# Cross attention's small matmuls on parts of the TensorE array: value products by head in turns, folded queries and text scores by head over 64 rows

## Chip, cores, metric

One core of a Trainium2 chip runs the kernel. The metric is device time in microseconds of one execution, median over runs.

## The reference, cut to what matters

The program is a two-layer block over x of 16 batches x 64 queries x 256 features and a context of 16 x 1601 x 256. In order, each with a residual sum: a deformable cross attention, a self attention, a mixture of 8 experts, a second cross attention, a state space scan, a mixture of 32 experts. Everything is float32. The change lies in the second cross attention alone:

```python
ctx_txt = context[:, :TEXT_LEN, :]            # 77 positions
ctx_img = context[:, TEXT_LEN:, :]            # 1524 positions
q = (x @ Wq).reshape(B, N, HEADS, DIM_HEAD)   # 16 heads of 64
k = (ctx_txt @ Wk).reshape(B, TEXT_LEN, HEADS, DIM_HEAD)
v = (ctx_txt @ Wv).reshape(B, TEXT_LEN, HEADS, DIM_HEAD)
out = _attend(q, k, v)                        # softmax(q k^T / 8) v
k_ip = (ctx_img @ Wk_ip).reshape(B, Li, HEADS, DIM_HEAD)
v_ip = (ctx_img @ Wv_ip).reshape(B, Li, HEADS, DIM_HEAD)
out = out + _attend(q, k_ip, v_ip)
return out @ Wo + bo
```

## The kernel before

Up to about 750 us the kernel projects the context's keys and values of the first attention, writes them to DRAM and gathers samples from them. From 753 us on the second cross attention runs (class `Cross`) and carries nearly all other stages beside it as "side" work: generators of the self attention, the first experts, the scan (`Ssm`) and the routing, of which a piece is issued at fixed places of each step. It ends at about 2690 us; the rest of the second experts follows. The order on PE, DVE and ACT is the order in which the program issues the instructions (`manual_schedule`); `tick` counts estimated microseconds of the program, not of the chip, to pace gathers.

The cross attention takes 128 steps (`step`), one for each batch b (16) and pair of heads hp (8). 128 columns of a step are 2 heads x 64 queries. The keys of the image positions are never projected. Instead the query is folded with the key weights, and the folded query is multiplied with the context itself:

- `queries` (L1009 on) projects the queries of two batches and writes them to `qbd`, a tile of 128 rows (two heads x 64 features) by [hp, batch of the two, head, query]. Each head writes only its own 64 rows (L1029); the other 64 rows of its columns stay zero from a memset (L1652). A matmul over 128 rows and 128 columns of it thus gives both heads at once.
- `fold(n)` (L1060 to L1072) makes the folded query of step n: for each of the two halves k of the 256 features one matmul (L1069), stationary 128x128 key weights `w`, moving 128 columns of `qbd`. Both halves lie in one PSUM bank `pf`; ACT copies it to `qf` (L1072).
- `step(n)` first issues the scores, `st` (helper `mm`, L88): 12 chunks of 128 positions, 2 matmuls each, in 3 banks of a pool of their own. DVE takes the maximum of each bank (L1144) and joins them (L1146). Between them stand the transposes of the step before last's output (`turn_out`, L153, ACT copy to `ot` L1122), then `out(n - 2)`, the first third of the product of the step before (`product`, L1113: 4 chunks, weights `pt`, moving 257 columns of context `cn`), the transpose of the maxima (L1163), DVE's maximum over it (L1165), side work, the second third, the transpose back (L1173), ACT's copy `mc` (L1175), `fold(n + 2)`, DVE's differences (L1184, L1187) and ACT's exponentials (L1185, L1188), and the last third of the product with its normalisation (L1194, L1196).
- `out(n)` (L1074 to L1089) is the value projection: for each head an accumulation of three matmuls into its own 64 partitions of one bank: text values times text probabilities (`vt`, `ptt`), then the two halves of `wvi` times `ot`. It is done by `mm` (L88), one head after the other. ACT copies the result to `yt` (L1089).
- `text(b, h)` (L1031 to L1048) makes the text scores of four pairs of heads, 32 times in all: four matmuls over 128 rows (stationary `qbd`, moving 77 keys, L1038) into one bank, from which DVE takes maximum (L1042) and difference (L1044); ACT takes the exponential (L1045), DVE normalises (L1046 to L1048). It is called at hp 5 and 6 of each batch, for the next batch. `text_turn` transposes the result a step later (L153, ACT L1058).

The banks of folds, text, transposes, products and side work come from one pool of 4 (`bank`); a new tile waits until the last reader of the tile that had its bank is done. The score banks (`big`) are another pool of 4.

Of the kernel before, what the change touches and what calls it, by code (L numbers as in the profile page):

```python
# [17 lines left out]
P = 128  # L18
B, S, D = 16, 64, 256
M = 1601  # L20
KC = D // P
# [13 lines left out]
H1, HD1, INNER, TEXT = 16, 64, 1024, 77  # L35
# [30 lines left out]
def perceiver_kernel(ctx: ExitStack, tc: tile.TileContext, a: dict, out: bass.AP):  # L66
    nc = tc.nc

    def mk(pool, shape, tag, dtype=F32, bufs=None):
        return pool.tile(list(shape), dtype, tag=tag, name=tag, bufs=bufs)  # L70
# [15 lines left out]
    def mm(o, pairs):  # L86
        for i, (l, r) in enumerate(pairs):
            nc.tensor.matmul(o, lhsT=l, rhs=r, start=i == 0, stop=i == len(pairs) - 1)  # L88
# [53 lines left out]
    def bank():  # L142
        return mk(pmm, [P, 512], "mm")
# [12 lines left out]
    def load(pool, tag, src, shape, bufs=None):  # L156
        t = mk(pool, shape, tag, bufs=bufs)
        nc.sync.dma_start(out=t, in_=src)
        return t
# [57 lines left out]
    qbds = []  # L217
# [51 lines left out]
    for j in range(2):  # L269
        r = slice(j * S, (j + 1) * S)  # L270
# [688 lines left out]
    class Cross:  # L959
# [71 lines left out]
        def text(self, b, h):  # L1031

            if b >= B:
                return
            kt, qbd, bb = self.kt[b], qbds[b // 2 % 2], b % 2
            ps = bank()[:, : 4 * TEXT].rearrange("p (i n) -> p i n", n=TEXT)
            for i in range(4):
                nc.tensor.matmul(ps[:, i, :], lhsT=qbd[:, h * 4 + i, bb].rearrange("p h q -> p (h q)"), rhs=kt[:, h * 4 + i, :],  # L1038
                                 start=True, stop=True)
            sh = [P, 4, TEXT]  # L1040
            mx = mk(small, [P, 4], "tmx")
            nc.vector.tensor_reduce(mx, ps, AX.X, ALU.max)  # L1042
            pe = self.pe[b, h] = mk(self.xp, sh, "pet", bufs=2)
            nc.vector.tensor_tensor(pe, ps, mx.unsqueeze(2).to_broadcast(sh), ALU.subtract)  # L1044
            nc.scalar.activation(pe, pe, AF.Exp)  # L1045
            nc.vector.tensor_reduce(mx, pe, AX.X, ALU.add)  # L1046
            nc.vector.reciprocal(mx, mx)
            nc.vector.tensor_tensor(pe, pe, mx.unsqueeze(2).to_broadcast(sh), ALU.mult)  # L1048
# [11 lines left out]
        def fold(self, n):  # L1060

            if n >= B * NHP:
                return
            b, hp = divmod(n, NHP)
            w = self.w[b, hp // 4]
            rhs = qbds[b // 2 % 2][:, hp, b % 2].rearrange("p h q -> p (h q)")
            pf = bank()
            for k in range(KC):
                nc.tensor.matmul(pf[:, k * P : (k + 1) * P], lhsT=w[:, hp % 4, k * P : (k + 1) * P], rhs=rhs,  # L1069
                                 start=True, stop=True)  # L1070
            qf = self.qf[n] = mk(self.xc, [P, KC, P], "qf", bufs=3)
            nc.scalar.copy(qf.rearrange("p c n -> p (c n)"), pf[:, : KC * P])  # L1072

        def out(self, n):  # L1074

            if n < 0:
                return
            b, hp = divmod(n, NHP)
            t, bb = divmod(b, 2)
            if t not in self.yt:  # L1080
                self.yt[t] = mk(self.xp, [P, NHP, 2, S], "yt", bufs=2)
            ot = self.ot.pop(n)
            py = bank()
            for h in range(2):
                r = slice(h * HD1, (h + 1) * HD1)
                cols = slice(hp * P + h * HD1, hp * P + (h + 1) * HD1)
                mm(py[r, :S], [(self.vt[b][:TEXT, cols], self.ptt[b][:TEXT, hp, r])]
                   + [(wvi[:, k, cols], ot[:, k, r]) for k in range(KC)])
            nc.scalar.copy(self.yt[t][:, hp, bb, :], py[:, :S])  # L1089

        def project(self, t):
# [506 lines left out]
    with tc.manual_schedule(engines={ET.PE, ET.DVE, ET.Activation}):  # L1598
# [21 lines left out]
        for s in range(B * 7 + 1):  # L1620
            run(kv)
            if s >= 1:
                run(early)
            if s == 14:
                pace["open"] = True
            tick(3.9)
            if s >= 18 and next(text, True) is None:
                tick(2.4)
            if s == 60:
                drain(text)  # L1630
                stx.close()
                tc.swap_default_side()
                slp = ExitStack()
                lp = slp.enter_context(tc.tile_pool(name="lp", bufs=2))
                tc.swap_default_side()
                mw = Middle(lp)
                for t0, nt in ((0, TG), (TG, ND0 - TG)):
                    mids += [(4 * (t0 + nt), attention(t0, nt, lp, mw)), (0, middle(t0, nt, lp, mw))]
                late = attention(ND0, 1, lp, mw)
                for k in range(KC):  # L1640
                    nc.vector.tensor_scalar(rws[:, k, :], rws[:, k, :], rsc[:, k : k + 1], None, ALU.mult)
            if lp:
                mid()
                if s < 94:
                    mid()
        drain(kv)
        skv.close()
        wvi = load(xw, "wvi", a["xwvi"].rearrange(kp, p=P), [P, KC, INNER])
# [10 lines left out]
        i = 0  # L1659
# [30 lines left out]
        for t in range(ND0 + 1, NPAIR):  # L1690
            i = (t - ND0) % TG
# [44 lines left out]
        i = 0  # L1736
# [127 lines left out]
```

## Time and profile before

| what | value |
|---|---|
| median of 3 runs | 2980.36 us (2976.62 to 2980.77) |
| the profiled execution | 2978.07 us, its span 2976.4 us |
| PE busy, of the span | 2811.3 us, 94% |
| DVE, ACT, POOL busy | 1626.4, 1071.7, 830.4 us |
| scores L88 st<-qf,cT | 6144 passes, 278 ns each |
| products L1113 | 3072 passes, 385 ns each |
| folds L1069 | 504 + 8 passes, 276 ns each |
| value products L88 | 512 passes mm<-ptt,vt of 246 ns, 1024 mm<-ot,wvi of 222 ns |
| text scores L1038 | 256 passes, 269 ns each |

How to read it: the profile is of one execution on the chip. Groups are named by line, engine and tiles, "out<-in" with buffer numbers left out. PE is the matmul stream, PEld the weight loads that run beside it. The trace has two matmuls ("passes") and two loads for each float32 matmul of the program, except for transposes, which have one. The ends of matmuls are modelled, so the 278 ns of a pass are its time in flight; where passes follow each other, the distance from start to start says what one costs. In a timeline a line is start, duration, engine, source line, tiles, shape and count; "[idle <- releaser]" is idle time before it and what ended it. A line of the waits is "engine line <- what it waited for: us in total, times, longest".

### The profile page before, as it was taken

What the parts mean: (1) busy time and instruction counts of PE and PEld (TensorE: products, weight loads), DVE (VectorE), ACT (ScalarE), POOL (GpSimd) and SP (SyncE); (2) the same over time, 40 slices, a digit from 0 to 9 for tenths busy, and PEclk for the clock granted to TensorE, in tenths of its full rate; (3) what the DMA queues carried; (4) which work ended last, traced back from release to release, by engine and by line L of the source; (5) the groups of instructions that cost most, each with busy time, mean ns of one, the idle gap of its engine ahead of it and who ended that gap; (6) DMA issues with size and microseconds to landing.
All of it is one profiled execution on the core that took longest, in us unless ns stands there. A gap on an engine that the chain in (4) does not pass through costs nothing.

```text
span 2976.4 us, 46295 instructions
## 1 busy us (share of the span) xinstructions
PE 2811.3 (94%) x17734; PEld 2344.9 (79%) x17734; DVE 1626.4 (55%) x4138; ACT 1071.7 (36%) x2427; POOL 830.4 (28%) x923
## 2 busy tenths in 40 slices
PE   8999999796899988999999999999999999997799
PEld 4554466464788877899999999999999999994687
DVE  3344443533566655332557754686544785655856
ACT  3443433542223443333343332443232443222431
POOL 0677777777771000000101100020000010001723
PEclk9999999998899999999999999999999999999999
DMA  7666766476322101465212111121111221005753
GB/s 218 180 193 201 225 184 195 137 236 183 77 69 63 49 10 41 135 192 167 70 50 80 52 33 52 55 71 55 38 33 47 66 64 51 8 1 161 218 151 110
DMA packets 324853, 313.97 MB, mean 105 GB/s; under 512 B 57989, under 2 KB 275881, under 8 KB 324121
## 3 DMA queue, kind: packets, MB, share of 16 engines
q1 hardware_dynamic: 172137, 213.05, 22.5%
q10 hardware_dynamic: 126928, 63.06, 7.5%
q0 software_dynamic: 25568, 34.91, 5.3%
q8 instruction: 141, 2.31, 0.3%
q14 instruction: 79, 0.65, 0.1%
HBM read 236.31 MB, written 74.62 MB: 104 GB/s over the span
## 4 chain that ended last, share of the span: by engine, by line
PE 76%; DVE 8%; POOL 6%; issue 3%; DMA 3%; ACT 3%; SPq 1%; ACTq 0%; DVEq 0%; POOLq 0%
PE st L88 31%; PE mm L1113 21%; PE mm L88 14%; POOL g L446 6%; PE mm L153 4%; PE mm L1069 2%; DMA g<-tab,ig 2%; DVE hs L1359 1%; PE mm L1099 1%; DVE hc L1364 1%; PE mm L1038 1%; ACT pt L1185 1%; DVE db L1357 1%; DVE mp L1144 1%; PE mm L1163 1%
## 5 line engine op out<-in xcount | busy, mean ns | idle before, releaser
L1113 PE MATMUL mm<-cn,pt 128*128 128x257 f32 (+1 forms) x3072 | 741.6, 385 | 1.2 <-ACT cT L82 1.2
L88 PE MATMUL st<-qf,cT 128*128 128x128 f32 x6144 | 739.9, 278 | 0.0
L88 PEld LDWEIGHTS st<-qf,cT 128*128 128x128 f32 x6144 | 721.3, 194 | 3.3 <-ACT qf L1072 0.2
L446 POOL DMA_INDIRECT g<-tab,ig x640 | 620.2, 969 | 282.1 <-issue 176.9
L1113 PEld LDWEIGHTS mm<-cn,pt 128*128 128x128 f32 (+1 forms) x3072 | 555.4, 190 | 84.6 <-ACT cT L82 2.3
L88 PE MATMUL st<-wkv,cxt 128*128 128x512 f32 (+1 forms) x832 | 377.1, 598 | 1.0 <-ACT cxt L415 1.0
L1144 DVE TENSOR_REDUCE mp<-st 128x128 f32<-128x512 f32 x384 | 260.4, 688 | 214.5 <-PE st L88 214.1
L1184 DVE TENSOR_TENSOR pt<-st,mc 128x512 f32<-128x512 f32 (+1 forms) x384 | 224.2, 639 | 152.2 <-ACT mc L1175 152.2
L88 PEld LDWEIGHTS st<-wkv,cxt 128*128 128x128 f32 (+1 forms) x832 | 149.1, 187 | 157.6 <-issue 155.9
L1185 ACT ACTIVATE pt<-pt 128x512 f32<-128x512 f32 (+1 forms) x384 | 207.5, 588 | 51.9 <-DVE pt L1184 51.6
L399 ACT COPY kv<-st 128x512 f32<-128x512 f32 (+1 forms) x208 | 121.3, 588 | 190.2 <-PE st L88 189.6
L1175 ACT COPY mc<-mm 128x128 f32<-128x128 f32 x128 | 34.2, 267 | 385.3 <-PE mm L1173 384.8
L972 POOL MEMSET cn<- 128x12 f32 x16 | 2.0, 122 | 590.6 <-PE mm L1113 584.1
L1122 ACT COPY ot<-mm 128x256 f32<-128x256 f32 x128 | 47.5, 371 | 311.2 <-PE mm L153 311.1
L1165 DVE TENSOR_REDUCE xmx<-mm 128x1 f32<-128x128 f32 x128 | 37.4, 292 | 193.4 <-PE mm L1163 193.4
L1465 POOL DMA_INDIRECT xb<-xnd,row x55 | 59.6, 1084 | 281.8 <-PE mm L1099 217.8
L1365 POOL TENSOR_TENSOR mn<-mn,hc 128x512 f32<-128x512 f32 x64 | 84.1, 1314 | 173.4 <-DVE hc L1364 165.2
L1089 ACT COPY yt<-mm 128x64 f32<-128x64 f32 x128 | 27.2, 213 | 248.4 <-PE mm L88 248.4
L88 PEld LDWEIGHTS mm<-xt,w 128*128 128x128 f32 x512 | 83.0, 197 | 26.0 <-issue 14.4
L88 PE MATMUL mm<-xt,w 128*128 128x256 f32 (+1 forms) x512 | 94.8, 333 | 3.3 <-DVE act L886 3.3
L1347 POOL MEMSET da<- 128x8 f32 x64 | 7.5, 117 | 319.3 <-ACT da L1346 319.0
L1359 DVE TENSOR_TENSOR_SCAN hs<-da,db 128x512 f32<-128x512 f32 x64 | 79.3, 1239 | 7.0 <-DVE db L1357 0.5
(469 smaller groups left out, 3978.1 us busy)
## 6 DMA issues: line engine op xcount, KB each, us to landing
tab<-kv ACTq DMA_DIRECT2D x48, 1024.0 KB
w<-in_gate SPq DMA_DIRECT2D x66, 512.0 KB
cx<-in_ctx SPq DMA_DIRECT2D x48, 512.0 KB
cn<-in_ctx SPq DMA_DIRECT2D x16, 1408.0 KB
w<-in_lin SPq DMA_DIRECT2D x33, 512.0 KB
wk<-in_xwkiT SPq DMA_DIRECT2D x32, 512.0 KB
wg<-in_guT SPq DMA_DIRECT2D x55, 256.0 KB
g<-tab,ig POOLq DMA_INDIRECT x640
```

The source lines that it names most:

```text
L88: nc.tensor.matmul(o, lhsT=l, rhs=r, start=i == 0, stop=i == len(pairs) - 1)
L153: nc.tensor.transpose(t[:ncol, i, :rows], b, ident[:rows, :rows])
L399: nc.scalar.copy(kv[:w, :, c, :], pk[:w].rearrange("p (h e) -> p h e", h=H0))
L446: nc.gpsimd.indirect_dma_start(out=gf[:, (half * n + s) * 4 * HD0 : (half * n + s + 1) * 4 * HD0], out_offset=None, in_=tables[j], in_offs ...
L1069: nc.tensor.matmul(pf[:, k * P : (k + 1) * P], lhsT=w[:, hp % 4, k * P : (k + 1) * P], rhs=rhs, start=True, stop=True)
L1113: nc.tensor.matmul(po, lhsT=pt[:w, c, :], rhs=cn[:w, c, :], start=c == 0, stop=c == NCH - 1)
L1144: nc.vector.tensor_reduce(mp_[:, i, :], s.rearrange("p c n -> p n c"), AX.X, ALU.max)
L1184: nc.vector.tensor_tensor(o, st[i][:, :m, :], mc.to_broadcast([P, m, P]), ALU.subtract)
L1185: nc.scalar.activation(o, o, AF.Exp)
L1359: nc.vector.tensor_tensor_scan(hs.rearrange("p c n -> p (c n)"), da.rearrange("p c n -> p (c n)"), db.rearrange("p c n -> p (c n)"), 0.0, ...
L1365: nc.gpsimd.tensor_tensor(y, y, hc, ALU.add)
L1465: nc.gpsimd.indirect_dma_start(out=x, out_offset=None, in_=xnd, in_offset=bass.IndirectOffsetOnAxis(ap=tb.row[:, i : i + 1], axis=0))
```

## The change

Three edits. The value products of the two heads are issued in turns, matmul by matmul, instead of head by head. The fold takes each head over its own 64 rows and 64 query columns (4 matmuls in place of 2), into a bank for each head, and ACT copies each bank to its half of `qf`. The text scores take each head over its 64 rows into its 64 partitions (8 matmuls in place of 4), into a bank for each head; ACT copies the two halves to SBUF, and DVE's maximum and difference read that copy. `qbd` and its zeros stay as they are. Lines behind the first edit move down by 5 or more: L1042 becomes L1048, L1069 L1076, L1072 L1080, L1113 L1123, L1144 L1154, L1163 L1173, L1173 L1183, L1175 L1185, L1185 L1195; the value products leave the helper and are L1098, their copy L1099, ACT's text copies L1045.

```diff
--- before.py
+++ after.py
@@ -1033,14 +1033,19 @@
             if b >= B:
                 return
             kt, qbd, bb = self.kt[b], qbds[b // 2 % 2], b % 2
-            ps = bank()[:, : 4 * TEXT].rearrange("p (i n) -> p i n", n=TEXT)
+            pe = ps = self.pe[b, h] = mk(self.xp, [P, 4, TEXT], "pet", bufs=2)
+            pb = [bank()[:, : 4 * TEXT].rearrange("p (i n) -> p i n", n=TEXT) for _ in range(2)]
             for i in range(4):
-                nc.tensor.matmul(ps[:, i, :], lhsT=qbd[:, h * 4 + i, bb].rearrange("p h q -> p (h q)"), rhs=kt[:, h * 4 + i, :],
-                                 start=True, stop=True)
+                for g in range(2):
+                    r = slice(g * HD1, (g + 1) * HD1)
+                    nc.tensor.matmul(pb[g][r, i, :], lhsT=qbd[r, h * 4 + i, bb, g, :], rhs=kt[r, h * 4 + i, :],
+                                     start=True, stop=True)
+            for g in range(2):
+                r = slice(g * HD1, (g + 1) * HD1)
+                nc.scalar.copy(ps[r], pb[g][r])
             sh = [P, 4, TEXT]
             mx = mk(small, [P, 4], "tmx")
             nc.vector.tensor_reduce(mx, ps, AX.X, ALU.max)
-            pe = self.pe[b, h] = mk(self.xp, sh, "pet", bufs=2)
             nc.vector.tensor_tensor(pe, ps, mx.unsqueeze(2).to_broadcast(sh), ALU.subtract)
             nc.scalar.activation(pe, pe, AF.Exp)
             nc.vector.tensor_reduce(mx, pe, AX.X, ALU.add)
@@ -1063,13 +1068,16 @@
                 return
             b, hp = divmod(n, NHP)
             w = self.w[b, hp // 4]
-            rhs = qbds[b // 2 % 2][:, hp, b % 2].rearrange("p h q -> p (h q)")
-            pf = bank()
+            pf = [bank(), bank()]
+
             for k in range(KC):
-                nc.tensor.matmul(pf[:, k * P : (k + 1) * P], lhsT=w[:, hp % 4, k * P : (k + 1) * P], rhs=rhs,
-                                 start=True, stop=True)
+                for h in range(2):
+                    r = slice(h * HD1, (h + 1) * HD1)
+                    nc.tensor.matmul(pf[h][:, k * S : (k + 1) * S], lhsT=w[r, hp % 4, k * P : (k + 1) * P],
+                                     rhs=qbds[b // 2 % 2][r, hp, b % 2, h, :], start=True, stop=True)
             qf = self.qf[n] = mk(self.xc, [P, KC, P], "qf", bufs=3)
-            nc.scalar.copy(qf.rearrange("p c n -> p (c n)"), pf[:, : KC * P])
+            for h in range(2):
+                nc.scalar.copy(qf[:, :, h * S : (h + 1) * S], pf[h][:, : KC * S].rearrange("p (k q) -> p k q", q=S))
 
         def out(self, n):
 
@@ -1081,11 +1089,13 @@
                 self.yt[t] = mk(self.xp, [P, NHP, 2, S], "yt", bufs=2)
             ot = self.ot.pop(n)
             py = bank()
-            for h in range(2):
-                r = slice(h * HD1, (h + 1) * HD1)
-                cols = slice(hp * P + h * HD1, hp * P + (h + 1) * HD1)
-                mm(py[r, :S], [(self.vt[b][:TEXT, cols], self.ptt[b][:TEXT, hp, r])]
-                   + [(wvi[:, k, cols], ot[:, k, r]) for k in range(KC)])
+
+            for i in range(1 + KC):
+                for h in range(2):
+                    r = slice(h * HD1, (h + 1) * HD1)
+                    cols = slice(hp * P + h * HD1, hp * P + (h + 1) * HD1)
+                    x, y = (wvi[:, i - 1, cols], ot[:, i - 1, r]) if i else (self.vt[b][:TEXT, cols], self.ptt[b][:TEXT, hp, r])
+                    nc.tensor.matmul(py[r, :S], lhsT=x, rhs=y, start=i == 0, stop=i == KC)
             nc.scalar.copy(self.yt[t][:, hp, bb, :], py[:, :S])
 
         def project(self, t):
```

## Prediction

> **What bounds the kernel now.** I read the windows first, then the waits, then the chain of work that ended last. All edits lie in the cross attention, which runs from 753 us to about 2690 us. The windows give busy time by stretch, in the order PE, PEld, DVE, ACT, POOL, then the clock:
>
> ```profile
> 1500.00:1700.00 200.00, 199.51 (x1494) 182.81 (x1493) 140.54 (x278) 71.38 (x180) 21.13 (x33) 1.00 0.18 54
> 1700.00:1900.00 200.00, 200.00 (x1484) 184.01 (x1483) 107.43 (x273) 70.91 (x163) 1.58 (x4) 1.00 0.16 51
> ```
>
> PE has no idle time there, its clock is granted in full, ACT is busy for 36%, DVE for 54 to 70%. PE's longest waits between 800 and 2690 us:
>
> ```profile
> PE mm L1163 <- DVE mp L1146: 7.5, 9, 2.5
> PE mm L153 <- DVE xn L103: 7.2, 2, 6.9
> ```
>
> All of PE's listed waits there come to some 35 us in 1890, so other engines can hide under 2% of a change on PE. The chain says the same of the whole span:
>
> ```profile
> PE 76%; DVE 8%; POOL 6%; issue 3%; DMA 3%; ACT 3%; SPq 1%; ACTq 0%; DVEq 0%; POOLq 0%
> ```
>
> So a nanosecond more or less of PE's sequence in a step of this loop is, 126 to 128 times, a nanosecond of the span; ACT and DVE matter only where PE comes to wait for them. As a busy PE in this profile only says that matmuls are in flight, I work with distances between starts.
>
> **The fold, before.** One float32 matmul stands in the trace as two passes, each a weight load and a matmul. The PE timeline around one fold:
>
> ```profile
> 1508.07 0.27 PE L1173 MATMUL mm<-ident,xmx 128*128 128x128 f32 x1
> 1508.17 0.61 PE L1069 MATMUL mm<-qbd,wk 128*128 128x128 f32 x4
> 1508.62 0.60 PE L1113 MATMUL mm<-cn,pt 128*128 128x257 f32 x2
> ```
>
> From the transpose (L1173) to the first pass are 108 ns, from there to the next product 446 ns (medians over the folds): 4 passes of 111 ns. Nothing drains, as all these matmuls take the whole 128x128 array.
>
> The change issues 8 passes in place of 4, each with 64 rows and 64 moving columns, but still 128 weight columns. Does a half-wide moving operand shorten a pass? The old text scores answer it: 77 moving columns over 128 weight columns.
>
> ```profile
> 1451.39 1.01 PE L1038 MATMUL mm<-kt,qbd 128*128 128x77 f32 x8
> 1452.24 0.60 PE L153 MATMUL mm<-ident,pet 128*77 128x128 f32 x4
> ```
>
> 8 passes in 849 ns, 106 ns each, hardly less than the 111 ns with 128 moving columns: the load of 128 weight columns sets the pass. Rows don't shorten a load either: 64 columns over 77 rows take 55 ns from start to start, over 128 rows 55 to 60. So a pass of the new fold still costs 106 ns, and the two heads must run side by side on the two halves of the array for 8 passes to cost what 4 did. Whether they do, and what it costs to enter and leave that shape, the trace shows at another place, the value products (L1088), which take 64 columns of the array at a time:
>
> ```profile
> 1501.77 0.83 PE L88 MATMUL st<-qf,cT 128*128 128x128 f32 x6
> 1502.53 0.33 PE L88 MATMUL mm<-ptt,vt 77*64 77x64 f32 x2
> 1502.70 0.22 PE L88 MATMUL mm<-ot,wvi 128*64 128x64 f32 x1
> 1502.70 0.27 PE L88 MATMUL mm<-ptt,vt 77*64 77x64 f32 x1
> 1502.76 0.22 PE L88 MATMUL mm<-ot,wvi 128*64 128x64 f32 x1
> 1502.81 0.22 PE L88 MATMUL mm<-ptt,vt 77*64 77x64 f32 x1
> 1502.81 0.45 PE L88 MATMUL mm<-ot,wvi 128*64 128x64 f32 x6
> 1503.19 0.70 PE L1113 MATMUL mm<-cn,pt 128*128 128x257 f32 x2
> ```
>
> Two things are to be seen. First, the second head starts at 1502.70 while the first still runs, and both then take 57 ns a pass: the column halves work at once. Second, a change of shape drains. The last full-array matmul starts at 1502.327; the first load of the 64-column shape follows at 1502.531, 204 ns later where 111 is the rule: 93 ns of drain, and the load (53 ns for 64 columns) is no longer hidden. On the way out the last 64-column matmul starts at 1503.043 and the product's load at 1503.193: 150 ns where 57 is the rule, again 93, and then the product's load of 107 ns stands bare (its second pass starts 321 ns after the first, not 217). The 32x32 matmuls at 1174.87 show the like: 100 ns from a 17-column matmul to the next full-array load.
>
> **The fold, after.** The new fold (L1076) changes shape in its middle of a full-array sequence, in and out, in all 126 folds of the loop. Counted from the transpose's start: load at 204, first matmul at 204 + 107 = 311, three more passes of 106 = 629, the other head beside it some 6 ns later (the two column halves at L291 start at 18.105 and 18.111), out after 53 + 93 = 781, the product's load of 107 = 888. Before it was 108 + 446 = 554. So **+334 ns a step, x126 = +42 us**.
> Bounds: a row split alone (64x128) is not in this trace, all switches shown change the columns too. If it drains nothing, the fold costs 4 x 106 in place of 446, -22 ns x126 = -3 us; nothing shorter, since 128-column loads set the pass. If it drains and the halves don't overlap, 4 more passes of 106 = +53 us on top, +95 us. I take +42, as every switch of shape in the trace drains.
> Here the Trainium skill speaks against the change: TensorEngine Tiling (Array Packing), Key Properties, says that a change of tiling mode, not of tile, drains TensorE, and it lists 64x128 as a mode. By the rule the sum holds +42; by these rows alone a row split could be -3.
>
> **The value products, after.** The heads alternate. In the old order the second head's first load comes 12 records behind the first head's and starts 171 ns later; at L291 it is 4 records behind and starts 6 ns later. The new order puts it 4 records behind. So the block shrinks from 340 + 171 = 511 ns (first to last start) to about 346: **-165 ns x128 = -21 us**. Nothing less than one head's own chain of 340 is possible, so -22 us is the floor; if the alternation brings nothing, 0. The switches on both sides stay.
>
> **The text scores, after.** 32 blocks, PE at 64 rows x 64 columns: 8 passes of 68 ns (77 columns of 0.83 ns, plus 4) = 544, plus 93 + 53 in and 93 + 107 out = 890 against 849: +41 ns x32 = **+1 us**. Without overlap +544 x32 = +17 more; without drains -10.
> ACT gets two copies of 64x308 (L539, the same width at 128 rows, takes 417 ns), and DVE's maximum (L1048) now waits for them: 0.83 us x32 = 27 us if all of it showed. Behind it on DVE stand the rest of the text's chain and the next step's maxima (L1154), for which PE waits at L1173 only some 8 us later. I take 0: that distance is the cover. DVE pays the same on SBUF as on PSUM (L1046 474 ns, L1042 474 ns). The two banks that wait for ACT are wanted next by the transposes of os, 16 passes later.
>
> **The exit of the fold.** Two copies to qf instead of one:
>
> ```profile
> L1072 ACT COPY qf<-mm 128x256 f32<-128x256 f32 x128 | 47.8, 373 | 18.6 <-PE mm L1069 7.9
> L1175 ACT COPY mc<-mm 128x128 f32<-128x128 f32 x128 | 34.2, 267 | 385.3 <-PE mm L1173 384.8
> L539 ACT COPY kts<-mm 128x308 f32<-128x308 f32 x32 | 13.3, 417 | 21.8 <-PE mm L88 21.8
> ```
>
> 2 x 267 - 373 = +161 ns, x128 = 21 us of ACT, behind which the exponentials (L1195) wait. They need DVE's first difference, which ends 1.30 us after the transpose; the second copy ends at about 1.38. Their result is wanted a whole step later. I take 0; at worst 21 us. In the built order the second bank of 6 folds was last read by the copy of mc (L1185), so those wait some 0.4 us: **+2 us**. SP and POOL issue the same transfers; one load of kt moves behind one of wq at the start, at no price, as both are loaded a step ahead.
>
> **Sum.** +42 - 21 + 1 + 2 = +24 us. The profiled execution took 2978.07 us (span 2976.4); the median of the three runs is 2.3 us above. 2978 + 24 + 2 = **3004 us**.
>
> **Rivals.**
> 1. The row split does not drain (faster). Mechanism: a 64-row load enters beside running full-array matmuls. Place: both ends of L1076. The fold falls from +42 to -3, the sum to -21, **2959 us**. It decides once entering and leaving cost under 170 ns a step together instead of 334 + 22. For it: no row of before has a pure row split. Against: each switch that it has drains. Chance 0.13.
> 2. The halves of rows don't overlap, or their weight loads go one after the other. The fold +95, the text +18: 3004 + 53 + 17 = **3074 us**; with the fold alone 3057. For it: overlap is shown for column halves only. Against: the Trainium skill, TensorE: Matmul & The Clock Gate, The mechanism, says that loads overlap running matmuls when their row groups differ; no run here shows that yet. Chance 0.2.
> 3. The copies on ACT come into PE's way: up to 27 + 21 us, **3025 to 3052 us**. For it: DVE is 70% busy in some stretches, so its slack is finite. Against: PE's 35 us of waits. Chance 0.1.
> 4. Draining, but with the next load already taken in: both 107 ns fall away, the fold is +15 us, the sum about -3: **2977 us**, no change. Against: the bare load behind every value product. Chance 0.07.
>
> **How the numbers follow.** My forecast has 0.5, with its own range 2993 to 3018; rivals 0.13, 0.2, 0.1 and 0.07. About 0.2% (6 us) is what a measurement of this kernel can tell from no change. Faster: rival 1, 0.13. Same: rival 4, 0.07. Slower: the rest, 0.8. The range reaches from rival 4 to rival 2 and leaves rival 1 out: 2976 to 3075.
>
> **What would show it.** Fold: from the transpose (L1183) to the first load 204 ns, to the next product's bare load some 780 ns; with 110 instead of 204, rival 1. Inside the fold two passes should start within some 10 ns of each other; passes 106 ns apart, eight in a row, are rival 2. Value products (L1098): both heads within 10 ns, 346 ns from first to last start. PE's waits for DVE at L1173 should stay near 10 us; 30 or more is rival 3. I am wrong altogether if a split pass takes another time than a full one.

## The result, and the profile after

| | before | after |
|---|---|---|
| median of 4 runs | 2979.03 us (2976.62 to 2980.77) | 3014.24 us (3009.39 to 3016.42) |
| the profiled execution | 2978.07 us, span 2976.4 | 3009.39 us, span 3007.7 |
| ratio after/before, 95% interval | | 1.0117 [1.0099, 1.0134] |

The change makes the kernel slower by some 35 us (30 to 40); forecast were 3004 us. The loop of the cross attention, taken from the first transpose back (L1183) to the last, grew by 36.5 us, so all of it lies there.

The windows of the kernel after, in the order PE, PEld, DVE, ACT, POOL, clock:

```profile
1500.00:1700.00 200.00, 197.97 (x1541) 176.42 (x1540) 134.04 (x270) 78.77 (x203) 18.42 (x30) 1.00 0.19 57
1700.00:1900.00 200.00, 200.00 (x1530) 179.04 (x1529) 109.29 (x267) 70.99 (x177) 4.28 (x7) 1.00 0.13 41
```

PE is still the bound and its clock still granted in full, but in the first stretch it is idle for 2 us, where it was 0.5. Passes rose from 1494 to 1541 and 1484 to 1530 per 200 us although the kernel is slower: there are more of them, of half the rows. The weight loads are busy for less time: after a change of shape nothing is loaded ahead.

**A fold.** PE, and then the weight loads, around one fold of the kernel after (start, duration, what):

```profile
1531.24 0.27 PE L1183 MATMUL mm<-ident,xmx 128*128 128x128 f32 x1
1531.44 0.66 PE L1076 MATMUL mm<-qbd,wk 64*128 64x64 f32 x8
1532.03 0.92 PE L1123 MATMUL mm<-cn,pt 128*128 128x257 f32 x3
```

```profile
1531.02 0.13 PEld L1183 LDWEIGHTS mm<-ident,xmx 128*128 128x128 f32 x1
1531.44 0.52 PEld L1076 LDWEIGHTS mm<-qbd,wk 64*128 64x128 f32 x8 [0.28 <-issue]
1532.03 0.73 PEld L1123 LDWEIGHTS mm<-cn,pt 128*128 128x128 f32 x4
```

Before, the fold's load ran under the transpose. Now the load unit stands idle for 0.28 us, and the first load of 64 rows begins 199 ns after the transpose has begun and its matmul 201 ns (medians over the loop). The eight matmuls come as four pairs: 7 ns apart within a pair, and from pair to pair 160, 112 and 112 ns. The last start is 391 ns behind the first one, the product's first pass 202 ns behind that. The whole takes 0.79 us from transpose to product, where it took 0.55.

**The value products**, in turns, of the kernel after:

```profile
1526.62 0.50 PE L88 MATMUL st<-qf,cT 128*128 128x128 f32 x3
1527.04 0.34 PE L1098 MATMUL mm<-ptt,vt 77*64 77x64 f32 x4
1527.21 0.40 PE L1098 MATMUL mm<-ot,wvi 128*64 128x64 f32 x8
1527.54 0.70 PE L1123 MATMUL mm<-cn,pt 128*128 128x257 f32 x2
```

Both heads' text products now stand side by side ahead of both heads' image products. From first to last start it is 347 ns (511 before); the switch in (205 ns) and out (152 ns) stays.

**A text step.** What the prediction took at nothing shows on DVE. First DVE in the same step of the kernel before (step 45, hp 5), from the end of the product of one step to the maxima of the next:

```profile
1553.78 0.49 DVE L1196 TENSOR_SCALAR os<-mm,xrc 128x256 f32<-128x256 f32 x1
1554.18 0.47 DVE L1042 TENSOR_REDUCE tmx<-mm 128x4 f32<-128x308 f32 x1
...
1560.17 0.29 DVE L1146 TENSOR_TENSOR mp<-mp 128x128 f32<-128x128 f32 x1
1560.95 0.29 DVE L1165 TENSOR_REDUCE xmx<-mm 128x1 f32<-128x128 f32 x1 [0.48 <-PE mm L1163]
```

then ACT and DVE in it, after:

```profile
1563.63 1.64 ACT L1195 ACTIVATE pt<-pt 128x512 f32<-128x512 f32 x3 [2.27 <-DVE pt L1194]
1565.18 0.29 ACT L1198 ACTIVATE pt<-pt 116x128 f32<-116x128 f32 x1
1565.38 0.83 ACT L1045 COPY pet<-mm 64x308 f32<-64x308 f32 x2
```

```profile
1564.97 0.48 DVE L1206 TENSOR_SCALAR os<-mm,xrc 128x256 f32<-128x256 f32 x1
1566.24 0.47 DVE L1048 TENSOR_REDUCE tmx<-pet 128x4 f32<-128x308 f32 x1 [0.79 <-ACT pet L1045]
...
1568.93 0.68 DVE L1349 TENSOR_TENSOR mt<-xc,dt 128x512 f32<-128x512 f32 x1
1569.54 0.61 DVE L1351 TENSOR_SCALAR mn<-xc,dp 128x256 f32<-128x256 f32 x2
...
1572.30 0.29 DVE L1156 TENSOR_TENSOR mp<-mp 128x128 f32<-128x128 f32 x1
```

and last PE's transpose of the maxima, before and after:

```profile
1560.61 0.30 PE L1163 MATMUL mm<-ident,mp 128*128 128x128 f32 x1 [0.24 <-DVE mp L1146]
```

```profile
1572.74 0.30 PE L1173 MATMUL mm<-ident,mp 128*128 128x128 f32 x1 [1.01 <-DVE mp L1156]
```

The two copies stand on ACT behind the exponentials; DVE sits idle for 0.79 us until they are done. From the start of its normalisation to the text's maximum it is 1.27 us (1564.97 to 1566.24), where it was 0.40 (1553.78 to 1554.18), and the scores' maxima come later by about as much. The side work of the scan (L1349, L1351) stands between and leaves no slack. PE waits 1.01 us for the maxima; in the same step before it waited 0.24. Over the loop, DVE's waits at the text (engine, line <- what it waited for: us, times, longest) and PE's longest wait, after:

```profile
DVE tmx L1051 <- ACT pet L1050: 24.0, 30, 1.9
DVE tmx L1048 <- ACT pet L1045: 23.5, 27, 1.6
```

```profile
PE mm L1173 <- DVE mp L1156: 13.3, 12, 3.4
```

The first stood at 15.8 us before, the second had no counterpart, the third stood at 7.5. PE's listed waits in the loop come to 46 us, 36 before.

### The profile page after: what moved, and what is told of

Read it like the earlier page. It is cut to its first block, busy times and chain, and to the rows that moved or that the text cites. A ratio compares the mean times of both kernels' runs of the same rounds, so it can differ in the third digit from the quotient of the medians.

```text
span 3007.7 us, 48085 instructions
## 1 busy us (share of the span) xinstructions
PE 2836.2 (94%) x18502; PEld 2322.7 (77%) x18502; DVE 1632.8 (54%) x4138; ACT 1107.6 (37%) x2619; POOL 825.3 (27%) x923
## 4 chain that ended last, share of the span: by engine, by line
PE 74%; DVE 9%; POOL 5%; DMA 4%; ACT 4%; issue 3%; SPq 0%; ACTq 0%; DVEq 0%; POOLq 0%
PE st L88 30%; PE mm L1123 21%; PE mm L88 12%; POOL g L446 5%; PE mm L153 4%; PE mm L1076 2%; PE mm L1098 2%; DMA g<-tab,ig 2%; DVE hs L1369 1%; DVE mp L1154 1%; ACT pt L1195 1%; PE mm L1109 1%; DVE hc L1374 1%; PE mm L1173 1%; DVE db L1367 1%
## 5 line engine op out<-in xcount | busy, mean ns | idle before, releaser
L1123 PE MATMUL mm<-cn,pt 128*128 128x257 f32 (+1 forms) x3072 | 752.4, 388 | 0.0
L1123 PEld LDWEIGHTS mm<-cn,pt 128*128 128x128 f32 (+1 forms) x3072 | 554.5, 190 | 90.1 <-issue 1.2
L1154 DVE TENSOR_REDUCE mp<-st 128x128 f32<-128x512 f32 x384 | 259.5, 688 | 212.3 <-PE st L88 212.1
L1195 ACT ACTIVATE pt<-pt 128x512 f32<-128x512 f32 (+1 forms) x384 | 207.2, 588 | 32.8 <-DVE pt L1194 30.1
L1185 ACT COPY mc<-mm 128x128 f32<-128x128 f32 x128 | 34.1, 266 | 387.5 <-PE mm L1183 387.0
L1175 DVE TENSOR_REDUCE xmx<-mm 128x1 f32<-128x128 f32 x128 | 37.4, 292 | 174.7 <-PE mm L1173 174.7
L1099 ACT COPY yt<-mm 128x64 f32<-128x64 f32 x128 | 27.2, 213 | 228.8 <-PE mm L1098 228.8
L1076 PEld LDWEIGHTS mm<-qbd,wk 64*128 64x128 f32 x1008 | 68.4, 187 | 36.2 <-issue 31.3
```

The source lines that it names most:

```text
L1076: nc.tensor.matmul(pf[h][:, k * S : (k + 1) * S], lhsT=w[r, hp % 4, k * P : (k + 1) * P], rhs=qbds[b // 2 % 2][r, hp, b % 2, h, :], start= ...
L1123: nc.tensor.matmul(po, lhsT=pt[:w, c, :], rhs=cn[:w, c, :], start=c == 0, stop=c == NCH - 1)
L1154: nc.vector.tensor_reduce(mp_[:, i, :], s.rearrange("p c n -> p n c"), AX.X, ALU.max)
L1195: nc.scalar.activation(o, o, AF.Exp)
```

## The experiments

All are built from the kernel before. Each group ran on one chip beside runs of the kernel before, and is compared with those. Only lines that differ are shown, with "..." where some are left out.

### Group 1: each part alone (before: 2975.91 us)

**e1_turns**: only the value products in turns.

```diff
-            for h in range(2):
...
-                mm(py[r, :S], [(self.vt[b][:TEXT, cols], self.ptt[b][:TEXT, hp, r])]
-                   + [(wvi[:, k, cols], ot[:, k, r]) for k in range(KC)])
+            for i in range(1 + KC):
+                for h in range(2):
...
+                    nc.tensor.matmul(py[r, :S], lhsT=x, rhs=y, start=i == 0, stop=i == KC)
```

> The kernel before with the value products in turns alone; fold and text scores as before. My theory (each edit's price is the change of PE's own sequence): from first to last start of a block 347 ns in place of 511, 164 ns x 128 steps = 21 us less, so about 2958 us against 2979. Rival theory A (PE has slack at this place, and what the turns save is waited away at the next transpose of the maxima): under 6 us less, 2973 or more.

Measured: 2957.71 us, ratio 0.9932 [0.9920, 0.9944], -18 us; the loop -18.7 us, -0.164 us a step. So this part alone is a gain, of the size that the start distances gave.

**e2_fold**: only the fold by head.

```diff
...
+                for h in range(2):
...
+                    nc.tensor.matmul(pf[h][:, k * S : (k + 1) * S], lhsT=w[r, hp % 4, k * P : (k + 1) * P],
+                                     rhs=qbds[b // 2 % 2][r, hp, b % 2, h, :], start=True, stop=True)
...
```

> The kernel before with the fold by head over 64 rows alone. My theory: drain in, drain out and one bare load of 107 ns, some 345 ns a step in 126 steps = +43 us, and 2 us for folds that wait for a bank: about 3024 us against 2979. Rival theory B (the fold is nearly free and the loss of the change sits in the text scores and in the copies on ACT): +10 us or less.

Measured: 3015.67 us, ratio 1.0133 [1.0118, 1.0147], +40 us; the loop +37.4 us, +0.34 us in a regular step. In seven steps at hp 2 and 5 it is 0.00; in all seven PE waits for the maxima (L1163) in the kernel before too. The fold alone is dearer than the whole change.

**e3_text**: only the text scores by head, with ACT's two copies.

```diff
...
+                for g in range(2):
...
+                    nc.tensor.matmul(pb[g][r, i, :], lhsT=qbd[r, h * 4 + i, bb, g, :], rhs=kt[r, h * 4 + i, :],
+                                     start=True, stop=True)
+            for g in range(2):
...
+                nc.scalar.copy(ps[r], pb[g][r])
```

> The kernel before with the text scores by head over 64 rows alone. My theory: +37 ns of PE in 32 blocks = +1 us, and +0.77 us in each block after which PE comes to wait for the maxima of DVE, which seemed about half of the 32 in the changed kernel: +10 us together, about 2989 us. Rival theory B: +20 us or more, as the text carries the loss. The prediction as made: +1 us.

Measured: 2993.24 us, ratio 1.0049 [1.0036, 1.0061], +17 us. The loop grew by 20.6 us: 9.2 at hp 5, 8.6 at hp 6, 2.7 at hp 0, all of it in the first step, and at most 0.3 at any other. Not every text step pays: 13 of the 32 did not grow. Its waits, DVE's for the copies and then PE's for the maxima and for a copy of DVE's:

```profile
DVE tmx L1048 <- ACT pet L1045: 23.3, 27, 1.8
```

```profile
PE mm L1168 <- DVE mp L1151: 13.2, 10, 3.2
PE mm L153 <- DVE cT L84: 3.5, 5, 1.9
```

The first two are those of the whole change, to 0.2 us: the chain copies, DVE, maxima, PE comes from this part alone. The third has no counterpart in the kernel before: at hp 6, PE waits for DVE to copy out transposed context (`cT`, L84), a second way in which a late DVE reaches PE.

**e4_fold_exit**: the old fold, but its bank copied by two ACT copies of 128x128.

```diff
-            nc.scalar.copy(qf.rearrange("p c n -> p (c n)"), pf[:, : KC * P])
+            for h in range(2):
+                nc.scalar.copy(qf[:, :, h * S : (h + 1) * S],
+                               pf[:, : KC * P].rearrange("p (k n) -> p k n", n=P)[:, :, h * S : (h + 1) * S])
```

> The kernel before; the fold's matmuls stay on the full array and in one bank, but ACT copies the bank to qf by head in two instructions, as the changed kernel does. My theory (ACT's 161 ns more a step are covered): within 3 us of 2979. Rival theory C (part of the fold's price is ACT's second copy, behind which the exponentials wait): up to 161 ns x 128 = +21 us, 3000.

Measured: 2976.94 us, ratio 1.0006 [0.9995, 1.0018]. The two copies of a step overlap in the trace: together they span 434 ns where one took 373, so ACT is busy for 8 us more in all (1080 for 1072), not for the 21 of the sum. These cost nothing that shows. So e2's +40 is PE's. That e3 pays for the place of its copies, ahead of DVE, is what e6_text_exit tests.

### Group 2: what the price hangs on (before: 2976.54 us)

**e5_fold_pairs**: the folds of two steps together, every second step. As many passes, half as many changes of shape.

```diff
-            if n >= B * NHP:
+            if n >= B * NHP or n % 2:
...
+            for j in range(2):
+                for k in range(KC):
+                    for h in range(2):
...
+                        nc.tensor.matmul(pf[h][:, c * S : (c + 1) * S], lhsT=w[r, (hp + j) % 4, k * P : (k + 1) * P],
+                                         rhs=qbds[b // 2 % 2][r, hp + j, b % 2, h, :], start=True, stop=True)
...
```

> The fold by head over 64 rows, but for two steps at a time in every second step: the same matmuls and copies as in the fold-only kernel, half as many changes of the array's shape. My theory (the price is paid for each change of shape): a pair takes 201 + 838 + 202 + 107 = 1348 ns plus 111 for the step without a fold, against 2 x 554 before: +351 ns a pair, +22 us, some 18 us less than the fold-only kernel (3016). Rival theory D (the price is paid for each pass, 8 small ones in place of 4): no gain by pairing, again +40 us.

Measured: 3000.9 us, ratio 1.0077 [1.0063, 1.0091], +24 us. PE in it:

```profile
2295.44 0.27 PE L1179 MATMUL mm<-ident,xmx 128*128 128x128 f32 x1
2295.64 1.11 PE L1072 MATMUL mm<-qbd,wk 64*128 64x64 f32 x16
2296.68 0.92 PE L1119 MATMUL mm<-cn,pt 128*128 128x257 f32 x3
```

Sixteen matmuls in a block between the same two gaps (201 and 202 ns). Half the switches, little more than half the price: it is paid per change of shape, not per matmul.

**e6_text_exit**: the old text matmuls, one ACT copy of 128x308 to SBUF, DVE reads the copy.

```diff
...
+            nc.scalar.copy(pe, ps)
+            ps = pe
...
```

> The kernel before with its full-array text matmuls in one bank; only the way out is new: ACT copies the bank to SBUF in one instruction of 128x308 and DVE reads that copy. My theory (the text's +17 us is the wait of DVE behind ACT's copies, and PE's wait for the maxima after it): one copy of 0.42 us in place of two of 0.41, so about half, +7 to +10 us, 2985. Rival theory E (the text's loss is PE's: 16 small passes and the change of shape): 0.

Measured: 2983.55 us, ratio 1.0027 [1.0016, 1.0038], +7 us, with PE's instructions as they were. DVE's waits for the copy:

```profile
DVE tmx L1045 <- ACT pet L1042: 13.7, 25, 1.4
```

One copy gives 13.7 us of DVE waiting and +7 us; two give 23.3 us and +17.

**e7_turns_2**: the value products in turns, of two steps at a time, into one bank, with one copy.

```diff
-            if n < 0:
+            if n < 0 or n % 2 != 1:
...
+            for j in range(2):
...
+                for i in range(1 + KC):
+                    for h in range(2):
...
+                        nc.tensor.matmul(py[r, j * S : (j + 1) * S], lhsT=x, rhs=y, start=i == 0, stop=i == KC)
...
```

> The value products in turns, for two steps at a time in every second step, into one bank with one copy; fold and text as before. My theory (each change of shape costs 93 ns and a bare load): a pair costs 1036 ns beyond the sequence without it, two single blocks in turns 2 x 699, so -362 ns a pair, -23 us below the turns-only kernel: about 2935 us. Rival theory A (steps without a block leave DVE less time for the maxima, and PE waits): 2950 or more.

Measured: 2937.56 us, ratio 0.9869 [0.9854, 0.9884], -39 us, the fastest version of all. PE in it, one block of 24 matmuls between two gaps:

```profile
2312.54 0.34 PE L1091 MATMUL mm<-ptt,vt 77*64 77x64 f32 x4
2312.70 0.40 PE L1091 MATMUL mm<-ot,wvi 128*64 128x64 f32 x8
2312.94 0.29 PE L1091 MATMUL mm<-ptt,vt 77*64 77x64 f32 x4
2313.05 0.40 PE L1091 MATMUL mm<-ot,wvi 128*64 128x64 f32 x8
```

It takes 205 ns in, 697 from first to last start, 152 out. Against e1_turns half the changes of shape are gone, worth another 20 us.

**e9_whole_array**: the value products on the whole array, both heads' columns in one matmul; twice the multiplications, half the output block unused, no change of shape; two ACT copies pick the halves.

```diff
+            mm(py[:, :P], [(self.vt[b][:TEXT, cols], self.ptt[b][:TEXT, hp, :])]
+               + [(wvi[:, k, cols], ot[:, k, :]) for k in range(KC)])
             for h in range(2):
...
+                nc.scalar.copy(self.yt[t][r, hp, bb, :], py[r, r])
```

> The value products on the whole array: 3 matmuls of 128 columns for both heads with 128 moving columns, half of whose output (one head's weights times the other head's values) is not used; ACT copies the two halves that are. Twice the multiplications, no change of shape. My theory: 6 passes of 111 = 666 ns beyond the sequence without it, against 864 before and 699 in turns: -198 ns x 128 = -25 us, about 2951 us, some 4 less than the turns-only kernel. Rival theory D (work counts, not changes of shape): no better than before, 2976 or more.

Measured: 2957.78 us, ratio 0.9939 [0.9925, 0.9952], -19 us. PE in it:

```profile
1630.69 0.39 PE L88 MATMUL mm<-ptt,vt 77*128 77x128 f32 x2
1630.92 0.61 PE L88 MATMUL mm<-ot,wvi 128*128 128x128 f32 x4
1631.37 0.82 PE L1113 MATMUL mm<-cn,pt 128*128 128x257 f32 x3
```

Six passes in place of twelve, with ordinary distances of 112 ns at both ends. Regular steps fell by 188 ns, 198 were foreseen; steps that wait for DVE gave less, which is the rest up to the 25 expected. Multiplying the zeros is as fast as leaving them out in turns, within a microsecond (e1_turns, in another group).

### Groups 3 and 4: how far the heads overlap

**e10_fold_heads** (before: 2977.77 us): the fold by head alone, as e2_fold, with the loops exchanged, one head after the other. The lines are shown against e2_fold.

```diff
-            for k in range(KC):
-                for h in range(2):
+            for h in range(2):
+                for k in range(KC):
```

> The fold-only kernel with the loops exchanged: all passes of the first head, then all of the second. My theory (the row halves work at once, as far as PE looks ahead: in the old value products the second head started when the 7th of the 12 records before its own went): the second head's first load is 9th in line and starts some 107 to 160 ns after the first head's, not 7, so the block takes 100 to 155 ns longer in 126 steps: +13 to +20 us over the fold-only kernel, 3029 to 3036 beside 3016 against 2976. Rival theory F (the halves overlap in any order): as the fold-only kernel, 3016. Rival theory G (without turns no overlap at all): 4 more passes of 106, +53 us.

Measured: 3014.24 us, ratio 1.0119 [1.0102, 1.0136], +36 us, and +0.347 us in a regular step where e2_fold had 0.340. The loads of one fold:

```profile
1616.79 0.53 PEld L1071 LDWEIGHTS mm<-qbd,wk 64*128 64x128 f32 x8 [0.28 <-issue]
```

The eight take 0.53 us, 0.52 in turns. The second head's first load starts 12 to 14 ns behind the first head's, although eight records stand ahead of it. I had expected the order to cost as it does in the value products; that fell.

**e11_wait_first**: the value products head by head as before, but the text's matmul last, so that a wait for the transposes stands at the first matmul of each head instead of the second. It ran on another chip, on which both kernels took longer (before: 3296.83 us); it is compared with that alone. In its trace the stage ahead of the cross attention takes some 250 us more than in the profile before.

```diff
-                mm(py[r, :S], [(self.vt[b][:TEXT, cols], self.ptt[b][:TEXT, hp, r])]
-                   + [(wvi[:, k, cols], ot[:, k, r]) for k in range(KC)])
+                mm(py[r, :S], [(wvi[:, k, cols], ot[:, k, r]) for k in range(KC)]
+                   + [(self.vt[b][:TEXT, cols], self.ptt[b][:TEXT, hp, r])])
```

> The kernel before with one head after the other as it was; within a head the text product comes last, so that the wait for ACT's copy to ot stands at the first of the 12 records of the first head and no longer at the third matmul pass. Theory H (PE looks only so far ahead: a load 9th in line was reached at once, one 13th in line is not): the second head starts some 170 ns after the first as before, the time stays at 2977. Rival theory I (the semaphore in the middle of the first head's chain holds up what is behind it): the second head starts within 20 to 60 ns, the block falls from 511 to 360 to 400 ns, -14 to -19 us, 2958 to 2963.

Measured: 3298.6 us, ratio 1.0003 [0.9976, 1.0031]. The weight loads of one block:

```profile
1938.74 0.36 PEld L88 LDWEIGHTS mm<-ot,wvi 128*64 128x64 f32 x6
1938.97 0.14 PEld L88 LDWEIGHTS mm<-ptt,vt 77*64 77x64 f32 x1
```

The first line holds four loads of the first head and, from the fifth on, two of the second head, which starts 171 ns behind, as before. So the wait in the middle was not the reason. With e10_fold_heads: a head whose first load is the 9th record in line starts at once, one whose first load is the 13th doesn't. But the two cases also differ in the kind of split, halves of rows there and halves of columns here, and no run separates this from the number of records. What sets the limit stays open.

## Why the prediction was right, and where a step of it failed

The sign and the size were right, by the mechanism that was given most of the chance. Of the terms of the sum, the text scores were put at next to nothing and cost 17 us; the others came out within 3 us.

- **The fold: right.** Foreseen were 204 ns to the first load, 629 ns to the last start, 781 to the product's load, 888 with the bare load; measured 199, 592, 791 and some 898. That is +340 ns a step for +334, +40 us for +42 by itself. The last start came sooner than foreseen (592 for 629), and the way out took longer: 202 ns from the last start to the product's first pass, where the value products leave their 64-column shape in 152. Both come from where the starts are recorded. In the full-array fold a pass starts 107 to 110 ns after its load has begun; in the split fold its start is recorded 2 ns (first pair) or 53 to 56 ns after it. The loads themselves are 108 to 112 ns apart, as foreseen. From the last load to the product's load it is 256 ns here (257 in e5_fold_pairs and e10_fold_heads) and 206 behind the value products, and the 50 ns between them are about what a load of 128 columns takes over one of 64 (107 for 53). So the length of the last load accounts for the longer way out.
- **The drain.** The row that stood for it (93 ns at each side of the value products) carried over to a split of rows alone. The Trainium skill, TensorEngine Tiling (Array Packing), Key Properties, says that a change of tiling mode drains TensorE; this trace agrees: 199 ns to the first load after a transpose, where 108 is the distance between starts without a change of shape. That 64 rows by 128 columns is such a change, no row of before showed. e5_fold_pairs shows that it is paid per switch.
- **The halves of rows overlap: right.** Pairs start 7 ns apart, so rival 2 is out. The Trainium skill, TensorE: Matmul & The Clock Gate, The mechanism, says that a load overlaps running matmuls of other row groups; the 7 ns agree.
- **Rival 1** (no drain, 110 ns to the first load) is out by the 199 ns. **Rival 4** (the next load already taken in) is out too: the product's second pass starts 321 ns behind its first, where it was 219, so that load stands bare as it does behind the value products.
- **The value products: right.** -165 ns a step foreseen, -165 measured by starts (868 to 703 ns from the last pass ahead of the block to the product's first, both switches included), -18 us by e1_turns for -21. Of the missing 3 us some 2 are 13 steps at hp 2, 5 and 6 that did not get shorter in e1_turns; in ten of them PE waits for the maxima (L1163) in the kernel before too.
- **The exit of the fold at nothing: right**, by e4_fold_exit, but cheaper to begin with: the two copies overlap, so ACT pays 61 ns more a step, not 161 (2 x 267 - 373 takes them one after the other). The six folds of which one head waits for a bank are there, at steps 27 to 29 and 121 to 123; at the last three it shows as +0.42 us each, 1.3 us for the 2 foreseen.
- **The text scores: wrong.** The step that failed is "PE waits at L1173 only some 8 us later … that distance is the cover". A distance between two instructions on different engines is no slack when the engine between them is busy. DVE fills those 8 us with the text's chain and the scan; in the step shown PE already waited 0.24 us before the change. The slack to look for stood in the same timeline: when the maxima were done against when PE wanted them. In an ordinary step that is 1.2 us (maxima at 1545.6, transpose at 1546.8), in the text step shown none. Where DVE has less to do the cover held: 13 of the 32 text steps of e3_text did not grow (at hp 5, DVE is busy for 5.5 to 9.3 us of these steps in the kernel before, and for 9.3 to 12.2 us of those that grew). Foreseen was +1 us for the whole part; e3_text measured +17 alone, and in the change the steps at hp 5 and 6 carry about 14 us of the 36.5 beyond what each step pays. That is rival 3, at somewhat over half of its first price (27). e6_text_exit shows one such copy at +7 with PE's work untouched. That the second copy accounts for the other 10 fits DVE's waits (13.7 to 23.3 us), but two copies with the old matmuls were not tried.
- **PE's own part of the text**, +41 ns foreseen, is nothing: text steps without a wait changed by -0.01 us. The passes took 68 ns as foreseen; the changes of shape came out some 50 ns cheaper than in the sum.
- **My mark for rival 3** (30 us or more of PE's waits at L1173) was blunt. The waits there rose only from 7.5 to 13.3 us; the rest shows at other lines (PE's listed waits +10 us together). Lengths of the steps by hp showed it at once.

The sum by parts alone: +40 - 18 + 17 = +39 us; together some +35, within the intervals of the three. By the loop's length it is 39.3 for 36.5 us, and 2.3 of the difference lie in the steps at hp 6; that parts share a wait there would fit, but was not shown. The prediction's sum of +24 lacked the text's 17 and had the rest about right.

## What to carry to other kernels

Price a matmul that uses part of the array by what a change of shape costs at both of its ends, and put such matmuls together or leave them at full size: here zeros that ride along in a full-width pass were cheaper than a fold without them, and one switch for two steps (e7_turns_2, -39 us) was worth more than any order within a step. Before a wait is taken as hidden, compare when the next consumer's input is ready and when it is wanted in the step that holds the new work, not in an average one. What a new copy costs depends on who waits for it, not on the engine that makes it: on the same ACT, 61 ns more in every step cost nothing (e4_fold_exit), while one copy of 416 ns every fourth step ahead of a busy DVE cost 7 us (e6_text_exit).

## What the runs showed of the hardware beyond the expected

- Each change between the full array and 64 columns costs 93 ns over the ordinary distance, in and out, and after it the first load stands bare (53 ns for 64 columns, 107 for 128). Entering the shape of 64 rows by 128 columns took 199 ns to the first load. Leaving it took 256 ns from the last load, for 206 from a last load of 64 columns; the two loads differ by about as much.
- Two row halves run 7 ns apart, and even head by head 12 to 14 ns, with eight records ahead (e10_fold_heads); with twelve records ahead and halves of columns the second head came 171 ns late (e11_wait_first and the kernel before).
- With 128 stationary columns a float32 pass takes 105 to 114 ns from start to start, be it over 64, 77 or 128 rows and with 64, 77 or 128 moving columns. Skipping zeros inside such a pass saves nothing.
